# Four hand-overs between the stages of an image kernel, rearranged on one core

## The chip, the cores and the metric

The kernel runs on one core of a Trainium2 chip. The metric is the time of one execution on the device in microseconds (us); the median of several runs is compared. The engines go by their short names: PE multiplies matrices (PEld are its weight loads), DVE and POOL work elementwise, ACT computes functions, and SP does nothing here but issue DMA transfers. POOL and ACT issue transfers too, each in the order of its own instructions.

## What is computed

The input `x` is an image of 256 by 256 pixels with 128 channels, float32. Four layers follow each other, each of the form "x plus a layer of the group norm of x":

```
def _gn(v, G=32, eps=1e-5):                     # mean and variance per group of 4 channels, over all pixels
    ...
x = x + _L0_conv_ref(_gn(x), ...)   # attention along rows, 4 heads, with a bias from the pixels
x = x + _L1_conv_ref(_gn(x), ...)   # gated complex recurrence, 16 steps: h = fg * (A h) + inp
x = x + _L2_conv_ref(_gn(x), ...)   # triangle product: left, right = gated projections of layer norm
                                    #   out = einsum('bikd,bjkd->bijd', left, right / L)
                                    #   out = sigmoid(pair_norm @ g_out) * (layer_norm(out) @ p_out)
x = x + _L3_conv_ref(_gn(x), ...)   # 3 x 3 convolution, 128 to 128 channels, then a 128 x 128 product
```

A group norm needs sums over the whole image. So no layer can start before the one ahead of it has finished its last pixel, and each hand-over ends in a short chain of tiny operations.

## The kernel before

**Stages.** Images lie in DRAM with channels as rows (128 partitions) and pixels as columns: `x1T` after attention, `x2T` after the recurrence, `x3T` after the triangle layer. A Python loop writes out an order of steps for each stage, with a lag for each step (software pipelining), and `pin` keeps the instructions of that order. What is not pinned is placed by a scheduler.

**Group norm** (`group_affine`, `mean_variance`). While a stage runs, it adds up sums and sums of squares (about a shift) per channel in `stats`. At the hand-over `mean_variance` adds these (`mv`), scales them and takes the variance; a product with `group` (1/4 inside groups of four channels) gives the group mean `pm`; the spread of the channel means is added (`d`, `v`); a second product `pv` gives the group variance; ACT takes the root (`sd`), after loading its table; `ab` holds the factor and the offset of the norm. `keep_busy` puts products of no use between these, so that PE does not stand idle.

**Recurrence.** 64 blocks of 1024 pixels, in an order of steps with lags 0 to 4. The 16 steps are done in closed form by four squarings; the tail of a block is: `xa`, `xb` (three products add up `g`, twice `dn8` and minus `tq16` in `pxb`), `be`, `e_`, `al` on DVE, `t1` on POOL, and then two transfers `ac1`, `ac2` issued by POOL, which add `t1` and `yf` into the tile `xc`. ACT then takes the sums of `xc` (`ev_`, `bn`: four instructions), and `st` stores the block to `x2T`. After the last block `red` adds up the sums and `partps` folds the halves.

**Triangle layer.** A first pass over 32 tiles of 2048 pixels takes the layer norm, stores it (`znT`), keeps the roots as rows (`rs2D`), and fills the gated projections `LR` of a first quarter of the channels. Then for each of four quarters `g`: 32 channels of products `z`, their results stored to `prodD`, while the sums for the second layer norm are kept in `sums` and `total`. The buffers are `X[0]` to `X[4]`, 2048 columns each; in this pass `X[4]` holds `shift`, `total` and `v`. `fetch(g + 1, n)` loads the first four tiles for the next quarter.

After the last quarter: `total` minus `v`, logarithm, exponential, into `rsm`, written to `rs3D`; `transformed_taps` (called by `prepare`) multiplies the convolution's taps with the 128 x 128 matrix (`cpk`) and makes the six combinations `U` from them.

**Output stage.** 32 tiles of 2048 pixels. For each tile: `pa` spreads a row of roots over all partitions (`ra`), `xs` normalises on DVE, `e0` and `e1` are the products `pe` of the halves, `sg` their sigmoid, `pb` spreads the second row (`rb`), `sc` scales the loaded `pd`, `y0` and `y1` are the products `py`, `gy` gates, `ad` adds to `x` on POOL (the last tile on DVE), `qu` takes the squares, `st` stores to `x3T`. Steps of the tile before have lag 1:

```
order = (
     (lx, 0), (pa, 0), (y0, 1), (y1, 1), (xs, 0), (lp, 0), (gy, 1), (e0, 0), (pb, 0), (ad, 1),
     (sc, 0), (e1, 0), (sg, 0), (qu, 1), (st, 1),
)
```

**Convolution.** 16 blocks of 16 rows, by a transform along the rows (four rows of output from six `v`, groups of four rows). ACT applies the norm (`normalise`, into `xp`), DVE makes the six `v` (`transform`), PE multiplies (`products`, tiles `m`, one bank each of eight), DVE and ACT combine them (`rows`). Transform `gs` selects groups of a block; the first block is made in two halves.

The lines of the profile that are named below: L61 is every product, L55 every ACT function, L958, L961, L964, L1073 and L1087 are the recurrence's helpers and its transfers, L1119 is the pinned helper of the triangle layer, L1382 loads the rows of roots, L1400 the tiles `x` and `pd`, and L1588 to L1603 the transform.

Of the kernel before, what the change touches and what calls it, by code (L numbers as in the profile page):

```python
# [31 lines left out]
class Kernel:  # L32
# [50 lines left out]
    def group_affine(self, pool, psum, stats, group, tag, whole=False, shift=None, mv=None, busy=8):  # L83

        nc = self.nc
        if mv is None:
            mv = self.mean_variance(pool, stats, tag, shift)
        pin = self.tc.keep_in_program_order
        pm = psum.tile([P, 2], F32, name=f"pm{tag}", tag="gn")
        self.keep_busy(psum, busy)  # L90
        pin(self.mm(pm[:, 0:1], group, mv[:, 0:1]))
        self.keep_busy(psum, 3)
        mg = pool.tile([P, 1], F32, name=f"mg{tag}")
        nc.vector.tensor_copy(mg, pm[:, 0:1])
        d = pool.tile([P, 1], F32, name=f"gd{tag}")
        nc.vector.tensor_sub(d, mv[:, 0:1], mg)
        v = pool.tile([P, 1], F32, name=f"gv{tag}")
        nc.vector.scalar_tensor_tensor(v, d, d, mv[:, 1:2], ALU.mult, ALU.add)
        pv = psum.tile([P, 2], F32, name=f"pv{tag}", tag="gn")
        pin(self.mm(pv[:, 0:1], group, v))  # L100
        self.keep_busy(psum, 3)
        sd = pool.tile([P, 1], F32, name=f"sd{tag}")
        self.chain("table", self.act(sd, pv[:, 0:1], AF.Sqrt, bias=self.eps))
        ab = pool.tile([P, 2], F32, name=f"ab{tag}")
        nc.vector.reciprocal(ab[:, 0:1], sd)
        nc.vector.scalar_tensor_tensor(ab[:, 1:2], mg, -1.0, ab[:, 0:1], ALU.mult, ALU.mult)
        if whole:
            return ab, mg, sd
        return ab

    def mean_variance(self, pool, stats, tag, shift):

        nc = self.nc
        mv = pool.tile([P, 2], F32, name=f"mv{tag}")

        nc.vector.tensor_reduce(mv, stats, AX.X, ALU.add)
        nc.vector.tensor_scalar_mul(mv, mv, 1.0 / NPIX)
        e = pool.tile([P, 2], F32, name=f"me{tag}")
        nc.vector.tensor_tensor(e[:, 0:1], mv[:, 0:1], shift, ALU.add)
        nc.vector.tensor_tensor(e[:, 1:2], e[:, 0:1], e[:, 0:1], ALU.mult)  # L120
        nc.vector.tensor_tensor(mv[:, 1:2], mv[:, 1:2], e[:, 1:2], ALU.subtract)
        return mv
# [28 lines left out]
    def constants(self, pool):  # L151
# [4 lines left out]
        self.g4 = self.load(pool, self.i["c_group4"], "g4")  # L156
        self.eps = pool.tile([P, 1], F32, name="eps")
# [146 lines left out]
    def later_weights(self, pool):  # L304
# [14 lines left out]
        W["bv"] = self.column(pool, I["L3_conv_bias"], "bv")  # L319

# [10 lines left out]
    def attention(self, wp, later, xT, x1T, znT, biasD, HD_, stats1, shift1):  # L331
# [5 lines left out]
        with ExitStack() as c:  # L337
# [7 lines left out]
            with self.pool(name="awq", bufs=2, space=PSUM) as ps0:  # L345
                ab, mg, _ = self.group_affine(wp, ps0, None, self.g4, "0", True, mv=mv)
                V.tensor_scalar_mul(shift1, mg, -1.0)
                lc, cb = self.centering(wp, ps0, ab, "0")
# [521 lines left out]
    def recurrence(self, x1T, x2T, HD_, stats1, shift1, stats2, shift2):  # L870
# [7 lines left out]
        with ExitStack() as c:  # L878
# [8 lines left out]
            with self.pool(name="rwp", bufs=2, space=PSUM) as ps0:  # L887
                ab, mg, _ = self.group_affine(wp, ps0, stats1, self.g4, "1", True, shift=shift1)
# [170 lines left out]
            def xb(d): total(d, "pxb", [[(self.ident, d["g"]), (twice, d["dn8"]), (negid, d["tq16"])]])  # L1059
            def lD(d): act(d["D"], d["D"], AF.Ln)  # L1060
            def eD(d): act(d["D"], d["D"], AF.Exp, bias=math.log(0.5), scale=-1.0)
            def be(d): stt(d["g"], d["pxb"][:, 0], 2.0, d["D"], ADD, MUL)
# [7 lines left out]
            def t1(d): gt(wide(d, "t1"), both(d["t"]), d["v"], MUL)  # L1070
            def yb(d): tt(d["yf"], d["yf"], both(d["g"]), MUL)

            def added(d, t): pin(nc.gpsimd.dma_start(d["xc"], t, accum_op=ADD))  # L1073
# [26 lines left out]
            for it in range(NB + deep):  # L1100
                for step, lag in order:
                    if 0 <= it - lag < NB:
                        D[it - lag]["b"] = it - lag
                        step(D[it - lag])
            red = wp.tile([P, 2, 2], F32, name="partsum")
# [646 lines left out]
```

## Time and profile before

| | us |
|---|---|
| median of 3 runs (4716.51 to 4721.29) | 4718.13 |
| time of the profiled execution | 4713.07 |
| its span, first to last instruction | 4711.2 |
| PE busy in the span | 4538.0 |
| DVE busy | 3746.5 |
| ACT busy | 3332.6 |
| POOL busy | 2104.2 |

The hand-overs that the change touches, by windows of the trace:

| hand-over | window (us) | PE busy | DVE busy | ACT busy | POOL busy | granted clock |
|---|---|---|---|---|---|---|
| attention to recurrence | 1651 to 1658 | 6.08 of 7 | 4.66 | 2.36 | 0.56 | 1.00 |
| recurrence to triangle | 2962 to 2999 | 12.73 of 37 | 11.79 | 9.84 | 12.20 | 0.63 |
| products to output stage | 3847 to 3880 | 21.73 of 33 | 12.98 | 9.75 | 8.44 | 0.64 |
| output stage to convolution | 4174 to 4188 | 13.94 of 14 | 9.93 | 8.49 | 1.14 | 1.00 |

The profile records one execution; times in it count from its first instruction. "Busy" of PE includes products that serve only to keep it busy. The granted clock is the share of its full clock that PE was given in a window. A row of the timeline has the start, the length, the engine, the line, the operation, output and inputs with their shapes, the number of instructions put together, and in brackets how long the engine had stood idle and what released it. Every float32 product stands in the trace as two instructions.

### The profile page before, as it was taken

How to read it: one execution, taken by the hardware profiler on the slowest of the kernel's cores; microseconds unless marked ns; L12 is line 12 of the kernel's file. 1: busy time of each engine (PE TensorE's matmuls, PEld its weight loads, DVE VectorE, ACT ScalarE, POOL GpSimd, SP SyncE). 2: the span in 40 equal slices, each digit the busy share in tenths (PEclk: the TensorE clock that was granted, in tenths of full speed). 3: DMA queues.
4: the chain of work that ended last, by engine and by line, in shares of the span. 5: the costliest groups of instructions: out<-in, count | busy, mean ns of one | idle time of the engine just before them, and what ended most of it. 6: DMA issues, size and time to landing. Idle time of an engine off the chain costs nothing.

```text
span 4711.2 us, 79401 instructions
## 1 busy us (share of the span) xinstructions
PE 4538.0 (96%) x30421; PEld 2602.1 (55%) x30421; DVE 3746.5 (80%) x4818; ACT 3332.6 (71%) x5176; POOL 2104.2 (45%) x1365
## 2 busy tenths in 40 slices
PE   8999999999999999999999999799999989999999
PEld 2444555555555533333333333356999963379999
DVE  6776777777777789999999999687666667789885
ACT  6555888888888889999999999698444444442210
POOL 0343555555555547666767666333231145520000
PEclk9999999999999999999999999899999989999999
DMA  8893122222222235555555555576767758955332
GB/s 306 298 348 147 46 82 84 88 82 86 82 84 88 69 92 135 135 131 129 136 131 131 134 129 121 188 258 238 250 218 254 259 191 312 356 220 173 131 115 72
DMA packets 221194, 769.14 MB, mean 163 GB/s; under 512 B 58726, under 2 KB 62076, under 8 KB 180468
## 3 DMA queue, kind: packets, MB, share of 16 engines
q1 hardware_dynamic: 154542, 465.37, 28.9%
q0 software_dynamic: 64976, 298.27, 22.1%
q8 instruction: 243, 3.98, 0.3%
q14 instruction: 137, 1.12, 0.1%
q10 hardware_dynamic: 1296, 0.40, 0.0%
HBM read 431.26 MB, written 265.55 MB: 148 GB/s over the span
## 4 chain that ended last, share of the span: by engine, by line
PE 65%; ACT 15%; DVE 11%; issue 6%; DMA 2%; POOL 1%; SPq 0%; ACTq 0%; POOLq 0%; DVEq 0%
PE z L61 14%; PE m L61 8%; PE nd L61 7%; PE sc L61 6%; PE ppq L61 3%; PE ppv L61 3%; PE pe L61 3%; PE zc L61 2%; PE py L61 2%; PE ppg L61 2%; PE ppk L61 2%; PE px L61 2%; ACT L933 2%; PE pr L61 2%; ACT x2q L55 2%
## 5 line engine op out<-in xcount | busy, mean ns | idle before, releaser
L592 DVE TENSOR_TENSOR e<-sc,bT 128x1024 f32<-128x1024 f32 x512 | 613.8, 1220 | 255.5 <-PE sc L61 253.4
L592 POOL TENSOR_TENSOR ks<-e 128x1024 f32<-128x1024 f32 x256 | 601.4, 2368 | 442.6 <-PE nd L61 429.2
L55 ACT ACTIVATE e<-e 128x1024 f32<-128x1024 f32 x512 | 539.4, 1054 | 39.1 <-DVE e L592 29.5
L61 PE MATMUL m<-U,v 128*128 128x128 f32 x4608 | 514.8, 275 | 0.0
L61 PEld LDWEIGHTS m<-U,v 128*128 128x128 f32 x4608 | 514.6, 192 | 0.0
L61 PEld LDWEIGHTS z<-wf,zt 128*128 128x128 f32 x4096 | 462.6, 192 | 54.0 <-DVE LR L1119 28.5
L61 PE MATMUL z<-wf,zt 128*128 128x128 f32 x4096 | 474.8, 277 | 6.0 <-DVE LR L1119 6.0
L1119 DVE TENSOR_TENSOR LR<-z,sg 128x512 f32<-128x512 f32 (+1 forms) x323 | 270.0, 867 | 165.5 <-ACT sg L55 165.5
L1119 POOL TENSOR_TENSOR zt<-zt,df 128x512 f32<-128x512 f32 x127 | 161.5, 1272 | 422.8 <-ACT df L55 422.6
L55 ACT ACTIVATE sg<-z 128x512 f32<-128x512 f32 (+1 forms) x323 | 160.9, 509 | 243.7 <-PE z L61 241.4
L61 PE MATMUL sc<-proj 32*128 32x256 f32 x4096 | 299.8, 403 | 3.2 <-DVE e L592 2.3
L961 POOL TENSOR_TENSOR fs<-f 128x512 f32<-128x512 f32 x64 | 176.3, 2755 | 275.4 <-DVE f L958 255.8
L61 PEld LDWEIGHTS sc<-proj 32*128 32x128 f32 x4096 | 187.9, 185 | 160.8 <-PE px L61 94.8
L61 PE MATMUL nd<-e,proj 128*32 128x256 f32 x4096 | 272.4, 384 | 2.6 <-DVE og L592 2.6
L55 ACT ACTIVATE dn<-dn 128x512 f32<-128x512 f32 x384 | 237.7, 619 | 10.3 <-DVE dn L592 6.3
L961 POOL TENSOR_TENSOR u<-t,tr 128x512 f32<-128x512 f32 x64 | 232.4, 3631 | 12.1 <-DVE tr L964 10.6
L961 POOL TENSOR_TENSOR t<-t,v 128x1024 f32<-128x1024 f32 x64 | 210.1, 3283 | 54.4 <-DVE t L958 54.4
L61 PE MATMUL z<-LR 128*128 128x256 f32 x1024 | 225.5, 383 | 7.5 <-DVE LR L1119 7.5
L1637 POOL DMA_DIRECT2D out_dram<-ys x32 | 37.0, 1157 | 424.2 <-DVE ys L1635 424.2
L1627 ACT COPY m4s<-m 128x512 f32<-128x512 f32 x32 | 18.7, 583 | 287.3 <-PE m L61 287.3
L61 PEld LDWEIGHTS z<-LR 128*128 128x128 f32 x1024 | 196.6, 192 | 35.6 <-DVE LR L1119 8.3
L1119 POOL TENSOR_TENSOR x<-ga,x 128x1024 f32<-128x1024 f32 x62 | 144.7, 2350 | 133.8 <-DVE ga L1119 133.8
(410 smaller groups left out, 10749.0 us busy)
## 6 DMA issues: line engine op xcount, KB each, us to landing
zt<-znT SPq DMA_DIRECT2D x96, 1024.0 KB
xin<-in_x_dram SPq DMA_DIRECT2D x48, 1024.0 KB
xr<-x3T SPq DMA_DIRECT2D x46, 768.0 KB
x1T<-x POOLq DMA_DIRECT2D x64, 512.0 KB, 4.9
xf<-x1T SPq DMA_DIRECT2D x64, 512.0 KB
xc<-x1T SPq DMA_DIRECT2D x128, 256.0 KB
xc<-t POOLq DMA_DIRECT2D x64, 512.0 KB, 4.6
xc<-yf POOLq DMA_DIRECT2D x64, 512.0 KB, 5.0
```

The costliest lines, as they stand in the source:

```text
L55: return self.nc.scalar.activation(out, in_, func, bias=bias, scale=scale, **kw)
L61: return self.nc.tensor.matmul(out, lhsT, rhs, start=start, stop=stop)
L592: pin = lambda f: lambda *a, **k: tc.keep_in_program_order(f(*a, **k))
L933: pin(nc.scalar.preload_act_table_set(want))
L961: pin(nc.gpsimd.tensor_tensor(out, a, b_, op))
L1119: pin = lambda f: lambda *a, **k: tc.keep_in_program_order(f(*a, **k))
L1627: nc.scalar.copy(m4, m[4])
L1637: nc.gpsimd.dma_start(out[row:row + 8].rearrange("r p t c -> p (r t) c"), ys.rearrange("p g k t c -> p (g k t) c"))
```

## The change

- **Group norms.** For the recurrence, the triangle layer and the convolution, one product of the raw sums with `g4n` (the group matrix divided by the number of pixels) gives both group means at once; the variance is taken from them on DVE. Scaling, one product and several tiny operations are gone. The first group norm stays as it was.
- **Recurrence.** For the last block alone, `xb` is done by two DVE operations, `t1` on DVE, and `ac1` and `ac2` are additions on DVE. After the loop stand 56 products of no use (`warm`).
- **Taps.** The products of the taps (`cpb`, `cpk`) move from the output stage's beginning to the triangle layer's (`tap_products`), in place of 11 products of no use; the copies go from ACT to DVE. `transformed_taps` keeps only DVE's combinations; it is called between steps of the output stage's first tile.
- **Output stage.** `fetch` of the last quarter loads the first four tiles of `x2T` into `X[0]` to `X[3]`, and the first row of roots into `X[4]` (`root`); the stage then goes on using `X`. The row of `rb` for the first tile comes from `v` in SBUF by four small transfers of POOL and ACT; the write of `rs3D` and the rows of tiles 1 to 3 follow. In the first tile `e1` comes ahead of `pb`. The last tile's `gy` and `ad` alternate by halves.
- **Convolution.** The first block is transformed in groups 0, 1 and then 2 and 3; DVE does three of the first six rows of its `xp`; the first half's products go group by group. Fewer products of no use stand ahead of it (22 and 13 for 26 and 26).

By the order of instructions of both kernels: DVE's queue has, in the last product steps of the triangle layer, two of the tap combinations between its additions, two more between the halves of the first `xs`, and the other nine ahead of the first `sc`. POOL's queue has two loads of rows between its last additions and two after them. SP's queue has the first `pd` ahead of the last store to `prodD`, and waits for `rs3D` ahead of `pd` 2 and 3.

```diff
+    self.g4n = pool.tile([P, P], F32, name="g4n")
+    nc.vector.tensor_scalar_mul(self.g4n, self.g4, 1.0 / NPIX)
...
+            V.tensor_reduce(mv, stats, AX.X, ALU.add)
+            self.keep_busy(psum, busy)
+            pin(self.mm(pm, self.g4n, mv))
+            self.keep_busy(psum, 3)
+            V.tensor_tensor(d, pm[:, 0:1], shift, ALU.add)
+            V.scalar_tensor_tensor(v, d, d, pm[:, 1:2], ALU.mult, ALU.subtract)
+            V.tensor_copy(mg, pm[:, 0:1])
+            self.chain("table", self.act(sd, v, AF.Sqrt, bias=self.eps, scale=-1.0))
...
+            def last(d): return d["b"] == NB - 1
+            def xb(d):
+                if last(d):
+                    stt(thin(d, "tr8"), d["dn8"], -2.0, d["tq16"], MUL, ADD)
+                    tt(d["g"], d["g"], d["tr8"], SUB)
+                else:
+                    total(d, "pxb", [[(self.ident, d["g"]), (twice, d["dn8"]), (negid, d["tq16"])]])
...
-            def t1(d): gt(wide(d, "t1"), both(d["t"]), d["v"], MUL)
+            def t1(d): (tt if last(d) else gt)(wide(d, "t1"), both(d["t"]), d["v"], MUL)
...
+            def added(d, t):
+                if last(d):
+                    tt(d["xc"], d["xc"], t, ADD)
+                else:
+                    pin(nc.gpsimd.dma_start(d["xc"], t, accum_op=ADD))
...
+            for _ in range(56):
+                pin(self.mm(warm[:, 0, :P], self.ident, self.cmat))
...
-                ab, mg, _ = self.group_affine(wp, ps0, stats2, self.g4, "2", True, shift=shift2, busy=11)
+                self.tap_products(ps0)
+                ab, mg, _ = self.group_affine(wp, ps0, stats2, "2", shift=shift2, busy=0)
...
                 def fetch(g, n):
-                    if g < G:
-                        zt[g, n] = X[n % 4]
-                        nc.sync.dma_start(zt[g, n], znT[:, n * 2048:(n + 1) * 2048])
+                    zt[g, n] = X[n % 4]
+                    nc.sync.dma_start(zt[g, n], (znT if g < G else x2T)[:, n * 2048:(n + 1) * 2048])
+                root = X[4][:, 1536:]
...
+                        if g == G - 1:
+                            nc.sync.dma_start(root[32 * n:32 * n + 1], rs2D[:, n * 512:(n + 1) * 512])
...
-                nc.gpsimd.dma_start(rs3D[0].rearrange("(p n) -> p n", p=P), rsm.rearrange("p a j b -> p (a j b)"))
-            quarters.close()
-            prepare(W["kt"], W["wd"], W["bv"])
...
-                for p in range(4):
-                    D[p]["p"] = p
-                    load_x(D[p])
                 roots(0, "ra", rs2D, nc.gpsimd)
-                roots(0, "rb", rs3D, nc.gpsimd)
+                R["rb", 0] = io.tile([P, 4, 512], F32, name="rb")
+                for k in range(4):
+                    (nc.gpsimd, nc.scalar)[k % 2].dma_start(R["rb", 0][32 * k:32 * k + 1, 0], v[k:k + 1])
+                nc.gpsimd.dma_start(rs3D[0].rearrange("(p n) -> p n", p=P), v)
+                for k in range(4):
+                    nc.gpsimd.dma_start(R["rb", 0][32 * k:32 * k + 1, 1:], rs3D[0].rearrange("(p k n) -> k p n", k=4, n=512)[k:k + 1, 1:4])
...
+                first = [(step, lag) for step, lag in order if not lag]
+                cut = next(n for n, (step, lag) in enumerate(first) if step is pb)
+                e1_at = next(n for n, (step, lag) in enumerate(first) if step is e1)
+                first.insert(cut, first.pop(e1_at))
...
+                            if not it and step is pb:
+                                prepare()
...
+    def tap_products(self, ps):
+        W, V = self.weights, self.nc.vector
+        kt, wd = W["kt"], W["wd"]
+        pb = ps.tile([P, 2], F32, name="cpb", tag="gn")
+        self.mm(pb[:, 0:1], wd, W["bv"])
+        V.tensor_copy(W["bw"], pb[:, 0:1])
+        for t in range(3):
+            pk = ps.tile([P, 3, P], F32, name="cpk")
+            for n in range(3):
+                self.mm(pk[:, n], kt[:, 3 * t + n, :], wd)
+            V.tensor_copy(kt[:, 3 * t:3 * t + 3, :], pk)
...
+                if blk == 0:
+                    s, t = parts[0]
+                    V.tensor_scalar(xp[:, (s + t) // 2:t, 1:N + 1], xr[:, (s + t) // 2:t, :], ab[:, 0:1], ab[:, 1:2], MUL, ADD)
+                    parts = [(s, (s + t) // 2), *parts[1:]]
...
+                one_by_one = blk + half == 0
+                for g, i in [(g, i) for g in range(2) for i in order] if one_by_one else [(None, i) for i in order]:
...
-            for gs in (slice(0, 2), slice(2, 4)):
+            for gs in (slice(0, 1), slice(1, 2), slice(2, 4)):
```

## The prediction

> **What bounds the kernel now.** I read the page first (busy shares and the slices of part 2), then the chain of waits in order of time to find where the tensor engine is not the thing that ends last, then the timeline and the clock windows of those places alone.
>
> ```profile
> span 4711.2 us, 79401 instructions
> PE 4538.0 (96%) x30421; PEld 2602.1 (55%) x30421; DVE 3746.5 (80%) x4818; ACT 3332.6 (71%) x5176; POOL 2104.2 (45%) x1365
> PEclk9999999999999999999999999899999989999999
> ```
>
> PE is busy 96% of the span, so nothing that shortens another engine inside a stage is worth much. The granted clock has two dips (slices 26 and 33): the hand-overs from recurrence to triangle and from its products to its output stage. All edits sit at hand-overs, so I cost four of them: A (1651 us, into the recurrence), B (2962 to 2999, out of it), C (3847 to 3880, into the output stage), D (4174 to 4188, into the convolution). From the timeline:
>
> ```profile
> 2968.95 0.86 POOL L1073 DMA_DIRECT2D xc<-yf  x1 [4.11 <-DMA xc<-t]
> 2973.86 3.26 POOL L961 TENSOR_TENSOR t<-t,v 128x1024 f32<-128x1024 f32 x1 [2.78 <-DVE t L958]
> 2982.45 0.86 POOL L1073 DMA_DIRECT2D xc<-yf  x1 [4.09 <-DMA xc<-t]
> 2987.24 0.63 ACT L55 ACTIVATE x2q<-xc 128x512 f32<-128x512 f32 x1 [10.32 <-issue]
> 2990.44 0.42 DVE L1106 TENSOR_REDUCE partsum<-parts 128x4 f32<-128x256 f32 x1 [15.53 <-ACT x2q L55]
> 2999.12 1.06 PE L61 MATMUL mn<-zt,tmeana 128*32 128x512 f32 x8 [0.25 <-DVE twbe L1154]
> 3862.77 3.69 PE L61 MATMUL ra<-ra,tones 1*128 1x512 f32 x8 [7.59 <-DMA ra<-rs2D]
> 3866.61 3.75 PE L61 MATMUL pe<-xs,twe 128*128 128x512 f32 x4 [0.15 <-DVE xs L1119]
> 3879.86 3.70 PE L61 MATMUL py<-pd,two 128*128 128x512 f32 x8
> 4181.94 4.57 ACT L55 ACTIVATE xp<-xr,ab 128x1536 f32<-128x1536 f32 x3 [0.77 <-DMA x3T<-x]
> 4187.84 27.33 PE L61 MATMUL m<-U,v 128*128 128x128 f32 x243
> ```
>
> B: the last block walks through POOL, two accumulating transfers and four ACT sums before anything can be normalised. C: PE waits for a row that lands 7.4 us after its issue, then works slowly up to the first py; from there py follows py every 9.4 us with PE full. D: the first xp ends two waits together, the coefficients `ab` (4181.71 + 0.16) and the last store (4177.77 + its 4.1 us to landing = 4181.9); products start 5.9 us later. The clock, by windows:
>
> ```profile
> 2960.00:2962.00 2.00, 1.94 (x5) 0.57 (x3) 1.19 (x3) 0.73 (x2) 0.75 (x1) 1.00 0.00 0
> 2962.00:2964.00 2.00, 0.00 (x0) 0.00 (x0) 2.00 (x2) 0.00 (x0) 1.70 (x2) 1.00 0.00 0
> 2964.00:2966.00 2.00, 0.00 (x0) 0.00 (x0) 1.97 (x4) 1.73 (x4) 0.84 (x1) 0.52 0.33 66
> 3876.00:3878.00 2.00, 2.00 (x4) 0.67 (x2) 0.40 (x1) 0.00 (x0) 0.00 (x0) 0.50 1.02 430
> 3878.00:3880.00 2.00, 2.00 (x10) 0.46 (x10) 0.02 (x1) 1.11 (x1) 0.00 (x0) 0.79 0.99 418
> 3974.00:4068.00 94.00, 94.00 (x321) 34.96 (x321) 73.20 (x80) 44.86 (x62) 52.32 (x30) 1.00 0.94 357
> ```
>
> (Columns: window, length, busy of PE, its loads, DVE, ACT, POOL; clock, DMA share, GB/s.) The clock is 1 or one half. A mean of 0.52 puts a fall at 2964.1, 0.79 a rise at 3878.8.
>
> **A: group norm of the recurrence.** On the path from the reduce at 1652.49: the scaling (0.17), one product stage (pv, 0.38), a copy and the waits between are gone; one product gives both columns, then two small DVE operations, then the root. Row by row: pm ends 1653.35, gd 1653.56, gv 1653.80; the root's table is there at 1653.75, so sd runs at 1653.85 instead of 1654.69. **0.8 us**. An xf/xc load or HD row could hide it: 0 to 1.
>
> **B: last block on DVE.** From xa at 2965.92: tr, g, be, e_, al are five DVE operations of 512 columns at 0.72 in a chain (pxb and its slow PE pass, 2966.66 to 2971.6, are gone), so al ends at 2970.1; t1, the first sum, yb and the second sum are four of 1024 columns at 1.24: xc is ready at 2975.1. But block 62 still goes by transfer: its sums start at 2973.75 and take four times 0.8, to 2976.95; those of block 63 follow to 2980.2. The reduce comes at 2980.2, not 2990.44: 10.2. Removed too: t1 on POOL, two DMA issues on its queue; stores move up. Behind it: the 56 warming products are 112 instructions of 0.112 (the 52 of 5.81 us), 2962 to 2974.5, so 6 us short; the clock falls before 2980. partps then runs at 2980.7, and the tap products now lie ahead of pm: 20 instructions and 2 of tpw at 0.213 (half clock) for 3.4 to 5.1 us, pm at 2985.5 to 2986.1. In before the filler cost the same (partps 2990.91, pm 2995.47). The three kt copies (0.47 each) on DVE end about with them. From pm to `ab` 1.5 instead of 2.2. Sum: first mn near 2988.9 instead of 2999.1: **10.2 us**, bounds 9 to 12. The first x2T tile is no wait: issued at the end of partps as before, and the rows of before leave it 7.8 us.
>
> **C: output stage.** Tiles 0 to 3 and the first root row lie in SBUF before the last z (3847.4). The chain is now: the sums, delayed about 0.5 by two tap operations and two row issues (0.52 each) put between DVE's and POOL's last additions; total minus v, which stands ahead of xs on DVE, ends at 3852.9 (was 3852.45); xs first half to 3854.2; two U operations (0.65); second half to 3856.1. pe first and second half now run back to back from 3854.3. Between ra (3849 to 3850) and this PE stands 4 us. [...] rb's row: v is ready at 3854.5; POOL issues two parts by 3855.7, ACT two after its table load by 3857. The trace bounds the landing by 4.2 us (x3T, quiet queues) and 8.2 (rb of before, crowded): 3860 to 3864; only pd tiles 0 and 1 move then, so 3861. U's remaining nine operations (4.5 us at 0.47 to 0.55) end on DVE at 3861: hidden by the row. rb to 3862.1, sc halves to 3864.1, ra of tile 1, py at 3863.2 instead of 3879.86: 16.7. Against it: rb of tile 1 comes by the rs3D round trip, write issued at 3856.3, landing 4.4 to 7.1 later, POOL's four issues, 4.2 to 8.2 more, wanted at 3868.6: 0 to 5 us, I take 0.7; SP waits for the same write ahead of pd 2 and 3, which are wanted only near 3880; and light windows may drop the clock once: 0.5. **15.5 us**, bounds 9 to 17.5. Copies of kw on ACT and the cpk pass (4 us) lay under the row's wait already: nothing.
>
> **D: into the convolution.** Interleaving makes DVE's last four operations end at 4176.96 instead of 4177.46; the last store is issued and lands 0.5 earlier, 4181.4. The group norm is shorter, `ab` at 4181.1, but xp must overwrite tiles that this store reads, as before, so 4181.4 stands. DVE: four U updates to 4182.05, its half of xp (768 columns, 0.55 by the rows of TENSOR_SCALAR), then tb, ta, tg, v at 258 columns, 0.34 each (516 take 0.61): first product 4184.1 instead of 4187.84, 3.7. Given back: DVE needs 24 small operations (8.2 us) for what took 12 (7.3); the second half's third and fifth bank are freed by the row sums of the first, and walking both queues row by row PE waits 1.3 us there. After that the 4608 m instructions run at 0.112. **2.4 us**, bounds 0 to 4.
>
> Sum: 0.8 + 10.2 + 15.5 + 2.4 = 28.9. The profiled execution took 4713.07 (span plus 1.9), so it would take 4684.2; the median of the three runs is 5.1 higher: 4718.1 - 28.9 = 4689.2, say 4689. About 0.2% (9.4 us) is what a measurement here can tell from no change.
>
> **The rivals.**
>
> Wait takes the place of wait (0.25): the rows for rb land as in the crowded row (8.2 us: 3864) and tile 1 waits for rs3D; PE is idle again, falls to half clock and does the first py slowly. C is then 9, D perhaps 1: total 21, 4697. For: 7.1 to 8.2 are this seam's own rows. Against: the four 1 MB tiles that crowded it are gone.
>
> Hand-back in several seams (0.07): B's statistics wait on block 62 longer, D is zero since the store decides. Total 12 to 18, near 4703. For: two of D's three waits end in that store. Against: PE, not the store, carries the 5.9 us after it.
>
> Everything warm (0.05): the clock holds, 33 or more, 4684.
>
> It does not do what it says (0.02): if SP held the x2T loads until the last z, tile 0 would land about 4.2 us after 3848.5, when xs is due anyway (3852.9), and the root row by its 7.4 at 3855.9: 3 us less, still the main case. Only if both long seams ended in a wait outside these rows would A and D be left, 3 us: 4715, inside 9.4.
>
> Slower (0.03): the output stage becomes transfer bound. It moves some 99 MB (32 x 3.15 less four tiles, plus xr); PE needs 32 x 9.4 = 301 us, so 329 GB/s. The middle stretch shows a DMA share of 0.94 at 357. If the new queue order, with pd 2 and 3 behind the rs3D wait, kept them below 293 GB/s, the stage would take 339 us and eat the gain and 9 more: about 4728. Against: PE is 94.00 of 94 there, 430 GB/s occurs, and four tiles leave the stage.
>
> Main case 0.58, total 24 to 33.
>
> **Numbers.** 4689 is the main case's. The range 4682 to 4700 takes in its bounds and the first rival, leaving out the hand-back's and slower ends. Faster 0.95 (all but the last two cases and the fringe), same 0.02, slower 0.03.
>
> **What would show it.** Right: the reduce of partsum 10 us closer to the last av; no row on POOL for block 63; pe back to back and the clock back to 1 before the first py; py about 16 us after the last z instead of 32; m about 14 us after the last py begins, instead of 17.6. Wrong: a DMA releaser of several us ahead of rb, a clock of 0.50 under py, m with holes in the first two blocks, or a py period above 9.4.

## The result and the profile after

| | before | changed |
|---|---|---|
| median, 4 runs each | 4717.32 (4714.15 to 4721.29) | 4687.17 (4686.27 to 4692.74) |
| profiled execution, its span | 4713.07, 4711.2 | 4687.51, 4685.7 |
| a second profile of each, its span | 4712.30, 4710.4 | 4682.89, 4681.1 |

The ratio is 0.9938, interval 0.9921 to 0.9955: 30.2 us less by the medians, where 28.9 was forecast. The two pairs of profiles give 25.5 and 29.3.

From the page of the changed kernel, its span, engine shares and clock slices:

```profile
span 4685.7 us, 79549 instructions
PE 4524.4 (97%) x30447; PEld 2603.2 (56%) x30447; DVE 3753.2 (80%) x4828; ACT 3329.8 (71%) x5173; POOL 2099.7 (45%) x1364
PEclk9999999999999999999999999999999999999999
```

The two dips of the clock are gone from the slices; falls of 6.8 us remain at both seams (2979.32 to 2986.15, 3842.89 to 3849.72), as shown below. The seams, in the timeline of the changed kernel:

```profile
2963.43 12.67 PE L61 MATMUL warm<-cmat,ident 128*128 128x128 f32 x112
2970.61 0.86 POOL L1077 DMA_DIRECT2D xc<-yf  x1 [4.11 <-DVE g L958]
2975.52 1.22 DVE L952 TENSOR_TENSOR xc<-xc,yf 128x1024 f32<-128x1024 f32 x1
2975.54 0.63 ACT L55 ACTIVATE x2q<-xc 128x512 f32<-128x512 f32 x1 [7.46 <-issue]
2981.95 0.42 DVE L1113 TENSOR_REDUCE partsum<-parts 128x4 f32<-128x256 f32 x1 [5.20 <-ACT x2q L55]
2990.02 1.07 PE L61 MATMUL mn<-zt,tmeana 128*32 128x512 f32 x8 [0.25 <-DVE twbe L1162]
...
3843.20 2.19 PE L61 MATMUL ra<-zt,tones 1*128 1x512 f32 x8 [4.81 <-ACT zt L55]
3846.67 5.20 PE L61 MATMUL pe<-xs,twe 128*128 128x512 f32 x8 [1.27 <-DVE xs L1126]
3852.55 1.32 PE L61 MATMUL rb<-rb,tones 1*128 1x512 f32 x6 [0.69 <-DMA rb<-zt]
3855.09 3.70 PE L61 MATMUL py<-pd,two 128*128 128x512 f32 x8
...
4151.22 5.18 PE L61 MATMUL busy<-cmat,ident 128*128 128x128 f32 x44 [2.20 <-DVE ga L1126]
4156.24 0.28 PE L61 MATMUL pm<-mv,g4n 128*128 128x2 f32 x2
4157.05 1.28 ACT L55 ACT_TABLE_LOAD   x1 [3.34 <-DVE mg L97]
4159.87 1.07 DVE L1591 TENSOR_SCALAR xp<-xr,ab 128x768 f32<-128x768 f32 x1
4162.34 3.28 PE L61 MATMUL m<-U,v 128*128 128x128 f32 x27 [1.46 <-DVE v L1613]
```

Block 63 has no row on POOL (2970.61 is the last transfer of block 62), and its last sum (2975.52 to 2976.74) is hidden behind block 62's statistics. PE waits 0.69 us for the row of `rb`, where it had waited 7.59 for that of `ra`. In D, PE's fillers and not the store now stand in front.

Seam by seam, both profiles of each kernel (C and D run to and from the start of a `py`; D ends with the start of the first `m`):

| stretch | before | changed | gain forecast | measured |
|---|---|---|---|---|
| A: reduce of `mv` to first `za` | 4.59, 4.60 | 3.77, 3.77 | 0.8 | 0.8 |
| A: the same reduce to first `av` | 39.86, 39.65 | 39.90, 39.92 | 0.8 | -0.2 |
| start of last but one to start of last `av` | 19.15, 19.21 | 22.01, 19.06 | 0 | -2.9, 0.2 |
| B: end of last `av` to first `mn` | 37.18, 37.29 | 26.43, 26.41 | 10.2 | 10.8 |
| C: end of last `z` to first `py` | 32.51, 33.26 | 16.69, 16.56 | 15.5 | 16.3 |
| first to last `py` | 290.34, 290.34 | 290.34, 290.34 | 0 (0.7 and 0.5 taken off in C) | 0 |
| D: last `py` to first `m` | 17.64, 17.64 | 16.91, 16.91 | 3.7 | 0.7 |
| first `m` to the end | 523.33, 523.32 | 523.40, 523.39 | -1.3 | -0.1 |

### The profile page after: what moved, and what is told of

It is laid out like the page before. It is cut to its first block, busy times and chain, and to the rows that moved or that the text cites. A ratio compares the mean times of both kernels' runs of the same rounds, so it can differ in the third digit from the quotient of the medians.

```text
span 4685.7 us, 79549 instructions
## 1 busy us (share of the span) xinstructions
PE 4524.4 (97%) x30447; PEld 2603.2 (56%) x30447; DVE 3753.2 (80%) x4828; ACT 3329.8 (71%) x5173; POOL 2099.7 (45%) x1364
## 5 line engine op out<-in xcount | busy, mean ns | idle before, releaser
L55 ACT ACTIVATE e<-e 128x1024 f32<-128x1024 f32 x512 | 539.4, 1054 | 39.2 <-DVE e L586 29.6
L1126 DVE TENSOR_TENSOR LR<-z,sg 128x512 f32<-128x512 f32 (+1 forms) x323 | 269.9, 866 | 165.4 <-ACT sg L55 165.4
L1126 POOL TENSOR_TENSOR zt<-zt,df 128x512 f32<-128x512 f32 x127 | 161.2, 1270 | 423.4 <-ACT df L55 423.4
L55 ACT ACTIVATE sg<-z 128x512 f32<-128x512 f32 (+1 forms) x323 | 160.7, 509 | 244.3 <-PE z L61 242.0
L55 ACT ACTIVATE dn<-dn 128x512 f32<-128x512 f32 x384 | 238.0, 620 | 10.2 <-DVE dn L586 6.1
L955 POOL TENSOR_TENSOR u<-t,tr 128x512 f32<-128x512 f32 x64 | 237.0, 3704 | 10.9 <-DVE tr L958 9.8
L1126 POOL TENSOR_TENSOR zt<-ga,zt 128x1024 f32<-128x1024 f32 x62 | 144.7, 2351 | 117.5 <-DVE ga L1126 117.5
```

Of the source, the lines that this page charges most:

```text
L55: return self.nc.scalar.activation(out, in_, func, bias=bias, scale=scale, **kw)
L955: pin(nc.gpsimd.tensor_tensor(out, a, b_, op))
L1126: pin = lambda f: lambda *a, **k: tc.keep_in_program_order(f(*a, **k))
```

## The experiments

Each run is the changed kernel with the edits that are shown or named, and its ratio is to the kernel before on the same chip; its seams are read from one profile. In the edits, `...` stands for what is left out. Below, "the changed kernel's" values are those of the table.

**B undone.**

```
-            def last(d): return d["b"] == NB - 1
+            def last(d): return False
-            warm = ...; for _ in range(56): ...
```

> The changed kernel, but the last block of the recurrence is finished as all others (pxb product, t1 on POOL, two accumulating transfers) and without the 56 warming products. Theory (the chain of the last block ends 10 us earlier, seam B carries 10.8 us): the reduce of partsum comes 15 to 18 us after the last av instead of 12.4 us earlier than that sum would have it, the first mn 37 us after the last av instead of 26.4, total slower than the changed kernel by 9 to 11 us, ratio to the kernel before about 0.996. Rival (statistics of block 62, which still go by transfer, set the end anyway, and the gain in B came from the shorter group norm): the first mn moves back by 3 us or less. On the recurrence itself, which took 4.2 us more in the changed kernel's profile than before: if the edits of the last block lengthen its drain, start of za to end of the last av returns from 1309.0 to about 1304.9; if it was only the phase in which the clock fell, it lies anywhere between 1303 and 1310.

Measured: 4702.46 (14 runs), ratio 0.9976 (0.9968 to 0.9984). The reduce of `partsum` came 28.84 us after the last `av` (18.36), not at 15 to 18 as written beforehand; in the kernel before it was 28.5. The first `mn` came 38.76 after it (26.43): B is worth 12.3 against a kernel that keeps everything else, 1.5 more than against the kernel before. Of the 1.5, 0.3 lie ahead of the reduce; for the rest the likely cause is that the tap products now stand in this seam, ahead of `pm`. The rival is out. The last `av` came 22.52 us after the one before, with the tail undone: the 2.9 us that the first profile lost there don't come from the edit. Over all twelve profiles with A changed this interval is either 19.06 to 19.22 (7 times) or 22.0 to 22.7 (5 times), and the same program gave 22.01 and 19.06: it varies from execution to execution. The clock goes with it: within this interval it was at half for 3.4 us in all seven short ones and in both profiles of before, and for 10.2 to 13.2 us in all five long ones. A window of the changed kernel's first profile, and the same of its second:

```profile
2952.00:2960.00 8.00, 4.77 (x9) 1.89 (x8) 5.39 (x6) 2.90 (x7) 1.71 (x3) 0.79 0.59 133
2952.00:2960.00 8.00, 6.64 (x19) 3.29 (x20) 6.56 (x10) 3.75 (x8) 1.77 (x3) 1.00 0.59 133
```

(Columns as in the prediction's windows; the clock is the third number from the end.) What starts the longer fall stays open. In the tail-undone profile the output stage took 6.4 us more too, of which below.

**C, tiles fetched late.**

```
-                        fetch(g + 1, n)      # and the rows of root, for the last quarter
+                        if g < G - 1: fetch(g + 1, n)
...
+                for n in range(4): pin(nc.sync.dma_start)(root[32 * n:32 * n + 1], ...)
+                for n in range(4): pin(nc.sync.dma_start)(X[n], x2T[...])
```

> The changed kernel, but the first four tiles of x2T and the first row of roots are fetched by SP after the last store of prodD, instead of a quarter ahead. With the tiles late, the scheduler also puts all combinations of taps ahead of the first xs on DVE. Theory of the prediction's second-last case (tile and row land about when xs is due anyway): first py 3 to 5 us later than in the changed kernel (19.7 to 21.7 us after the last z instead of 16.7). Rival (the early fetch is what seam C lives from): row and tile land 7 to 8 us after their issue, PE falls to half clock, first py 10 us or more later.

Measured: 4694.89 (6 runs), ratio 0.9961 (0.9949 to 0.9974). First `py` 23.14 us after the last `z`, 6.5 later, and 5.3 more lost in the first two tiles: 11.8 in all. In the timeline of this kernel:

```profile
3842.63 2.86 PE L61 MATMUL ra<-zt,tones 1*128 1x512 f32 x8 [6.01 <-DMA zt<-rs2D]
3858.48 2.35 DVE L1126 TENSOR_TENSOR pd<-pd,rb 128x1024 f32<-128x1024 f32 x2 [9.00 <-DMA pd<-prodD]
3859.76 6.52 PE L61 MATMUL py<-pd,two 128*128 128x512 f32 x8 [3.67 <-DVE pd L1126]
```

`ra` starts only 1.2 us later than in the changed kernel (idle 6.01 for 4.81). The first `xs` then begins 10.4 us after the last `z` for 6.9, straight behind the tap combinations, which the scheduler put ahead of it here. What the prediction missed is the next wait: the four tiles of 1 MB are issued ahead of the second part of the first `pd`, DVE waits 9.00 us for it, PE stands 3.67 us, and `py` runs at half clock (6.52 for 3.70). So early fetch carries most of C. How much of the 11.8 is the 4 MB in the way of `pd` and how much the changed order on DVE, this run does not separate. Neither theory had either.

**C, row of `rb` by the round trip.**

```
-                    (nc.gpsimd, nc.scalar)[k % 2].dma_start(R["rb", 0][32 * k:32 * k + 1, 0], v[k:k + 1])
...
-                    ... R["rb", 0][32 * k:32 * k + 1, 1:], rs3D[0]...[k:k + 1, 1:4]
+                    ... R["rb", 0][32 * k:32 * k + 1], rs3D[0]...[k:k + 1, 0:4]
```

> The changed kernel, but the row of rb for the first tile comes through rs3D as before: write, then four loads, all on POOL. Theory (the row is what PE waits for last in seam C, so its route is on the path): write lands about 5.3 us after its issue, loads 5 to 8 us after theirs, the row at about 3858 to 3860 on the changed kernel's scale instead of 3852.55: first py 6 to 10 us later, with the clock at half under it since PE then stands idle for over 5 us. Rival (the round trip is hidden by xs, pe and the combinations of taps on DVE): first py at most 2 us later.

Measured: 4693.82 (5 runs), ratio 0.9961 (0.9947 to 0.9975). PE waited 2.33 us for the row, first `py` 19.39 us after the last `z`, 2.7 later: between the 6 to 10 of the theory and the 2 of the rival. Then that `py` took 6.72 instead of 3.70, so 5.7 in all. The route is on the path, but half of its price is the clock. The write took its 5.3 us; the loads, for which I had 5 to 8, were there 2.4 us after the first was issued.

**D, fewer fillers; B, more warming.**

```
-  self.group_affine(..., "3", shift=shift3, busy=22)     +  busy=4
-            for _ in range(56):                          +            for _ in range(80):
```

> The changed kernel with two edits at two seams: 4 instead of 22 products of no use ahead of the group norm of the convolution (seam D), and 80 instead of 56 warming products after the recurrence (seam B). D, theory (the fillers wait for a PSUM bank that the last gy holds, start 2.2 us late and stand in front of pm): pm about 2 us earlier, first m 14.7 to 15.2 us after the last py begins instead of 16.9. D, rival (the last store's landing at 4156.9 or the load of the root's table decides): first m moves by 0.3 us or less. B, theory (the clock falls at 2979.7 because PE stands idle for 6.3 us after the warming products): with 80 the clock stays at full, the tap products take 0.113 each instead of 0.15 to 0.21, first mn 24.7 to 25.2 us after the last av instead of 26.4. B, rival (DVE's copies and statistics set pm): 0.3 us or less.

Measured: 4685.91 (4 runs), ratio 0.9945 (0.9928 to 0.9961). D: `pm` 8.65 us after the last `py` begins (10.81), first `m` 15.15 (16.91), as the theory has it. The late-fetch kernel adds to it: there, from the same source line, the 44 filler instructions began at once behind the last `py`, without the wait for `ga`, and `m` came at 14.91. B: first `mn` 24.71 us after the last `av` (26.43), also as the theory has it. But that gain was given back: from the last `av` to the last `z` it was 874.21 (first profile of the changed kernel 874.81, second 874.28).

**C, rows of tiles 1 to 3 from `v`; D, table ahead.**

```
-  nc.gpsimd.dma_start(R["rb", 0][32 * k:32 * k + 1, 1:], rs3D[0].rearrange(...)[k:k + 1, 1:4])
+  nc.gpsimd.dma_start(R["rb", 0][32 * k:32 * k + 1, 1:], v[4 + k:16:4])
...
+  tc.keep_in_program_order(self.table("sqrt_and_others"))      # ahead of the convolution's group norm
```

> The run with 4 fillers and 80 warming products, and two edits more. Seam C: the rows of rb for tiles 1 to 3 come straight from v in SBUF as tile 0's does, not through rs3D. Theory (two of four executions with this code lost 3 to 6 us in the first two tiles of the output stage, because the row of tile 1 came late by the round trip or PE then fell to half clock): the rows land within 6 us of their issue, before 3856 on the changed kernel's scale, every py period is 9.4, 290.3 us from first to last py. Rival (the loss comes from the phase of the clock windows alone): a period of 12 or more can still occur. Seam D: the table of the root is loaded ahead of the group norm. Theory (load and root stand between gv and ab, 1.3 us): ab 1.2 us earlier, and then the last store's landing, 4.1 us after its issue, sets xp: first m 14.0 to 14.3 us after the last py begins instead of 15.15. Rival (the updates of U and the DVE half of xp set the end, the table does not): 15.0 or more.

Measured: 4684.5 (4 runs), ratio 0.9932 (0.9911 to 0.9954). No wait for a row, all periods 9.4. D: 15.28, no gain on the 15.15 of the run with 4 fillers and 80 warming products, though the root (`sd`) was done 1.3 us before the reciprocal ran. The timeline of this kernel:

```profile
4154.22 0.29 ACT L55 ACTIVATE sd<-gv,eps 128x1 f32<-128x1 f32 x1 [0.20 <-DVE mg L97]
4155.64 0.29 DVE L1571 COPY bw<-cpbw 128x128 f32<-128x128 f32 x1 [1.12 <-PE cpbw L61]
4155.85 0.15 DVE L111 RECIPROCAL ab<-sd 128x1 f32<-128x1 f32 x1
```

The reciprocal is queued on DVE behind a copy that waits for PE: the wait removed on ACT is replaced by one that had lain under it.

**C, `e1` behind `pb`; D, first block in two groups (with 4 fillers).**

```
-                first.insert(cut, first.pop(e1_at))
...
-            for gs in (slice(0, 1), slice(1, 2), slice(2, 4)):
+            for gs in (slice(0, 2), slice(2, 4)):
```

> The changed kernel with 4 fillers, and two parts undone at two seams. Seam C: e1 of the first tile after pb, as in the other tiles. Theory (in the changed kernel the second half of pe fills the wait for the row of rb): PE stands idle for about 3 us ahead of rb, half clock follows, first py 1.7 to 5 us later than 16.7. Rival (pe of the second half fits under the scaling of pd just as well): within 0.5 us. Seam D: the first block of the convolution in two groups of two, as before, products not group by group. Theory: tb, ta, tg and v at 516 columns take 0.6 each instead of 0.34, first m 1.0 to 1.2 us later than 15.15, the rest of the stage unchanged (523.4). The prediction's give-back (PE waits 1.3 us in the first block for the small groups): the rest of the stage gets shorter by 1 us or more, the sum of both unchanged.

Measured, one run: 4695.5. C: 22.25, 5.6 later, more than the theory's 5; PE waits 2.46 us for the row, then the second half of `pe` runs at half clock behind it (3.78 for 4 instructions). D: first `m` at 17.07, 1.9 later than 15.15, and the rest of the stage unchanged (523.39). The operations of 516 columns cost 0.61 each, and the scheduler put one other (`tc`) among the four, ahead of the `v` that the first `m` waits for. So the small groups bring 1.9 with that order, and the give-back of 1.3 doesn't exist.

**D, first `xp` on ACT alone (with 4 fillers).** The five lines of `if blk == 0:` in `normalise` are left out.

> The changed kernel with 4 fillers, and all of the first xp on ACT as before (DVE's half undone). Theory (DVE's half takes 1.07, not 0.55, and stands behind the updates of U, so ACT alone would be done as early): first m within 0.3 us of 15.15 after the last py begins. The prediction's reckoning (half of it on DVE at 0.55): first m 0.7 to 1 us later.

Measured, one run: 4683.56; first `m` at 15.11, for 15.15 with DVE's half. That part of the change brought nothing there.

**All of it, and both kernels again.** Beside the edits of the last runs, the tap combinations are pinned behind `xs`, the fillers are 11, and the copy of `bw` follows the updates of `U`.

```
-            V.tensor_tensor(e, k0, k2, ADD)        +            pin(V.tensor_tensor(e, k0, k2, ADD))   # and so on
+            tc.add_manual_dep(V.tensor_copy(bw, pbw).ins, upd.ins.name, NOSYNC, reason="bw")
```

> All that the runs so far point to, in the changed kernel: 80 warming products; rows of rb for tiles 1 to 3 straight from v; the combinations of taps pinned behind both halves of the first xs, so that none of them delays the last sums; 11 fillers ahead of the group norm of the convolution (they then end about when its statistics are ready), the table of the root loaded ahead, and the copy of the convolution's bias product behind the updates of U, so that it no longer stands in front of ab on DVE. Theory: B 24.7 us from the last av to the first mn (26.4 in the changed kernel), C 15.4 to 15.9 from the last z to the first py (16.7), D 14.0 to 14.5 from the last py to the first m (16.9): 5 to 5.5 us faster than the changed kernel, median about 4682 on the scale where that has 4687, ratio 0.9988. Rival (the rb row and the last store set C and D whatever DVE and ACT do): C 16.5, D 15.2, 3.5 us faster.

> The changed kernel once more, unaltered, for a second profile and a median beside the run before it. Seams as in its first profile (A 3.8, B 26.4 to 26.6, C 16.5 to 17, D 16.9). The recurrence, start of za to end of the last av: anywhere in 1305 to 1311 if the phase of the clock sets its drain; within 1 us of the first profile's 1309.0 if the program sets it. Output stage from first to last py: 290.3, or up to 6 us more if the row of the second tile comes late.

> The kernel before once more, unaltered, for a second profile. If the recurrence's length varies from execution to execution by the phase of the clock, it differs from the first profile's 1304.86 by more than 0.5 us, and lies within 1304 to 1311 like those of the changed one; if the changed kernel made it longer, it is again 1304.5 to 1305.3. Seams B 37.2, C 32.5 and D 17.6, each within 0.5 us except C, where the clock was at half and may move it by up to 3 us.

Measured on one chip: 4681.43 (4679.71 to 4683.46, 5 runs) for the version with all edits, ratio to before 0.9929 (0.9916 to 0.9943); 4684.88 (4682.89 to 4688.07, 5 runs) for the changed kernel again, 0.9938 (0.9924 to 0.9951). It is 3.4 us faster by the medians, within what the two overlapping intervals leave open. B 24.73, C 15.46 and D 14.39 came as expected, 5.4 together, but the first tiles of the triangle layer took 2.8 longer. The timeline of this version behind its first `mn`, and windows of the clock:

```profile
2983.80 1.07 PE L61 MATMUL mn<-zt,tmeana 128*32 128x512 f32 x8 [0.25 <-DVE twbe L1162]
2985.63 2.09 PE L61 MATMUL pr<-mr,tspread 32*128 32x512 f32 x8 [0.77 <-ACT mr L55]
2987.65 1.94 PE L61 MATMUL mn<-zt,tmeana 128*32 128x512 f32 x8
```

```profile
2984.00:2986.00 2.00, 1.24 (x12) 0.37 (x8) 0.00 (x0) 0.60 (x1) 0.00 (x0) 0.79 1.00 422
2986.00:2988.00 2.00, 2.00 (x12) 0.35 (x12) 0.24 (x1) 0.00 (x0) 0.00 (x0) 0.50 1.03 434
```

With 56 warming products the clock falls under the wait and is back up for these tiles (`pr` 1.14 in the changed kernel's second profile, all windows of 2984 to 2998 at 1.00); with 80 it holds through the seam and falls at about 2985.2, under the tiles: fourth `mn` 19.9 us after the first instead of 17.1. In D the last wait is now the store (`xp` on ACT: `[1.90 <-DMA x3T<-zt]`).

The recurrence of the kernel before took 1304.29 in its second profile (first 1304.86), 0.6 less: too little to show by itself that it varies there; both have the short last interval. The changed kernel's second took 1305.68 for 1309.04, and has it short now. So of the 4.2 us that its first profile lost between first `za` and last `av`, 2.9 are that interval in one execution, and 0.8 are A's, below. In the ten profiles with A changed and no products added there, the same stretch took 1305.3 to 1311.1, so two profiles of before are too few to say that the change costs nothing there.

**The clock at A and B.** Three products of no use more at A; then 80 warming products and three more at B.

```
                 ab, mg, _ = self.group_affine(wp, ps0, stats1, "1", shift=shift1)
+                self.keep_busy(ps0, 2)
...
                     V.tensor_scalar_mul(gw[g], raw, ab[:, 0:1])
+                self.keep_busy(ps0, 1)
```

> The version with all edits, with 56 warming products again, and three products of no use more at seam A: two after those behind pm, one ahead of the first za, where PE waits 0.5 and 0.3 us. In all profiles of the changed kernel the way from the statistics' reduce at A to the first av took 39.7 to 40.3 us, as before (39.7 and 39.9): the 0.8 us of the shorter group norm were lost again, za taking 1.7 instead of 1.1 and m 3.8 instead of 3.4 at half clock. Theory (with one product stage gone, its fillers are gone too, and the clock falls near 1655 instead of 1660): with three more products the clock holds to 1658 or beyond, first av 39.0 to 39.3 us after the reduce. Rival (a wait of the first blocks for HD rows or ACT sets the first av): 39.7 or more. At B: 26.4 to the first mn, and 874.3 us from the last av to the last z, 1 us less than the 875.3 of the version with all edits. Total 1 to 2 us below that version.

> As the run with three more products at A, but with 80 warming products, and two more of no use ahead of pc and one ahead of the first mn. In the three runs with 80 warming products the first mn came 1.7 us earlier, and the last z no earlier (874.2 to 875.3 us after the last av, against 872.9 to 874.8): the clock fell near 2985, under the first tiles. Theory (the window before 2985 holds too little full-width work; three products of 0.23 raise it): the clock stays at full under the first three tiles, fourth mn 17.1 us after the first, 872.5 to 873 us from the last av to the last z. Rival (three products are too few, or the fall comes later instead): fourth mn 18 to 20 us after the first, 874 to 875.5.

Measured on one chip (before: 4711.10): 4681.42 (4680.72 to 4684.0, 5 runs) and 4684.15 (4677.92 to 4694.31, 5 runs), both ratio 0.9938 (0.9924 to 0.9951 and 0.9952). Windows of the clock at A, first of the kernel before, then of the changed kernel's first profile, then of the first run with three more products:

```profile
1660.00:1662.00 2.00, 2.00 (x4) 0.42 (x2) 0.00 (x0) 1.51 (x2) 0.00 (x0) 0.55 0.06 9
```

```profile
1654.00:1656.00 2.00, 1.70 (x13) 0.46 (x10) 0.77 (x6) 0.00 (x0) 0.00 (x0) 0.74 0.59 191
1656.00:1658.00 2.00, 0.86 (x3) 0.50 (x2) 0.00 (x0) 1.66 (x2) 0.00 (x0) 0.50 0.06 7
1658.00:1660.00 2.00, 2.00 (x3) 0.68 (x2) 0.00 (x0) 1.56 (x2) 0.00 (x0) 0.50 0.04 4
```

```profile
1654.00:1656.00 2.00, 1.08 (x5) 0.25 (x4) 0.12 (x2) 0.84 (x1) 0.00 (x0) 1.00 0.24 65
1656.00:1658.00 2.00, 1.77 (x4) 0.68 (x4) 0.00 (x0) 1.98 (x3) 0.00 (x0) 1.00 0.05 5
1658.00:1660.00 2.00, 2.00 (x11) 0.71 (x12) 0.00 (x0) 1.62 (x3) 0.00 (x0) 1.00 0.25 54
```

In the first run the first `av` came 37.05 us after the reduce instead of 39.9, 2.9 us earlier than in the changed kernel and 2 more than its theory had. The second run has the same three products, and there it came 44.11 us after the reduce:

```profile
1656.85 3.68 PE L61 MATMUL busy<-cmat,ident 128*128 128x128 f32 x16 [2.86 <-issue]
```

PE stood 2.86 us for nothing that the profile shows, and the clock was at half from 1657.0 on under these fillers (1.95 us in the changed kernel). From the first `za` to the first `av` it took 35.8 us there, 33.0 in the first run and 36.1 in the changed kernel. So the gain of 2.9 is one profile's, and not repeated. In the kernel before the clock fell too, at about 1660.2.

At B the second run had its fourth `mn` 17.1 us after the first, with the first at 24.42: the clock held. But the last `z` came 875.7 after the last `av`, not 872.5 to 873: from the fourth `mn` to the last `z` it took 834.2 us, for 831.3 and 830.8 in the changed kernel, and the clock fell three times for 3.4 us there, for two times in those. The first run missed its figures for B as well (first `mn` 26.91, last `z` 878.7). In the totals no gain shows: both profiles had a long last interval of the recurrence (22.6, 22.7), the first fell under the triangle layer's first tiles (fourth `mn` at 19.7), and both under the first `py` (5.3 for 3.7); the second's execution was the slowest of its five. Which of these versions is the fastest stays open.

## Why the prediction was right, and where not

**Total.** The main case came, but that 28.9 lies so near 30.2 is in part luck, since errors cancel: by the means of both profiles B and C brought 27.1 for a forecast of 25.7, A and D 0.6 for 3.2. The spans of the profiles differ by 27.4 on average, and the stretches add up to that: 27.7 at the four seams and 2.0 from attention's end, less 1.8 between first and last `av` and 0.4 in the triangle layer. No edit aims at attention's end: its last statistics came 1.7 and 2.3 us earlier than in both profiles of before (1652.49), but over the other profiles with the change at anything between 1649.4 and 1655.7. Whether the edits move it stays open; what the medians show beyond 27.4 is in no profile.

**A.** The step "so sd runs at 1653.85 instead of 1654.69: 0.8" was right, its place on the path was not. The stage removed had taken its fillers with it, and the clock fell near 1655 instead of 1660: 4.2 us behind the reduce instead of 7.7. `za` and `m` lost what the norm had won. I had costed the removed fillers at nothing and looked for the cover in transfers. That the fillers are the cause rests on the windows and on one profile with three of them put back; the other profile, with its stall, does not show it.

**B.** The chain came as worked out: reduce 10.1 earlier, set by block 62's statistics and then block 63's, as forecast. They began 4.9 us after the transfer's issue at 2970.61, and DVE was done while they ran. The clock fell at about 2979.3, in the wait, as forecast:

```profile
2978.00:2980.00 2.00, 0.00 (x0) 0.00 (x0) 0.00 (x0) 1.94 (x5) 0.24 (x1) 0.83 0.85 262
```

It came back at about 2986.15, so the tap products ran at half clock for 3.4 us (from 2982.73), where the forecast had 3.4 to 5.1.

That the last block's chain carries B, and not the shorter group norm, is shown by the run with the tail undone, for the chain and the warming products together. The norm's own part was not tried alone.

**C.** The clock fell at about 3842.9, `pe` began at half clock and took 5.20 for eight instructions, and the clock was back to 1 at about 3849.7, before the first `py` (3855.09), as forecast.

```profile
3842.00:3844.00 2.00, 0.80 (x4) 0.61 (x8) 0.00 (x0) 1.94 (x3) 1.19 (x1) 0.72 0.62 189
```

The prediction has PE stand 4 us behind `ra`; it stood 1.3 there (3845.39 to 3846.67). `ra` was placed 1.7 us behind the last `z` and came 4.8 behind it (`[4.81 <-ACT zt L55]`), so PE stood still ahead of `ra` and not only behind it, 4.5 us by the time of the fall. In the kernel before, the fall at 2964.1 had come 2.1 us after the end of PE's last product (2961.94). In the first run with three more products at A it fell at about 3838.7, 2.0 us after the last `z` had ended at 3836.65:

```profile
3836.00:3838.00 2.00, 0.65 (x3) 0.22 (x2) 1.31 (x3) 1.35 (x4) 1.68 (x2) 1.00 0.94 193
3838.00:3840.00 2.00, 0.00 (x0) 0.00 (x0) 1.22 (x2) 0.65 (x2) 1.80 (x3) 0.67 0.64 213
```

So at these three falls PE had stood still for 2.0 to 4.5 us. In the changed kernel the clock came back 3.0 us after `pe` began. Mis-sized: the two tap operations and issues delay the sums by 1.3 us, not 0.5, since DVE's `e` and `h` took 0.92 and 1.06 beside POOL's addition, for 0.56 and 0.36 in the kernel before; with them pinned away C was 1.1 shorter. The row of `rb` landed 14.2 us after the last `z`, for 13.6 forecast. The terms 0.7 and 0.5, for tile 1's row and for the clock, are averages over cases that either come or don't. The 0.5 was the author's estimate, and no run shows it; in its place, in the five profiles with seam C as changed the way from first to last `py` is 290.3 four times, and 296.7 once (tail undone). The rival "does not do what it says" was under-priced: late tiles cost 11.8 us, not 3.

**D.** Forecast 2.4, measured 0.7. The failing step is "`ab` at 4181.1 [...] so 4181.4 stands", that the store decides. Counted from the start of the last `py`, the store landed as forecast (11.45 us for 11.2), but `ab` came at 13.65 for 10.9. The step left out the fillers. In the kernel before the `gy` of the first half released them, 3.4 us after that start:

```profile
4173.53 5.88 PEld L61 LDWEIGHTS busy<-cmat,ident 128*128 128x128 f32 x52 [0.57 <-DVE ga L1119]
```

In the changed kernel they waited for the last `gy` (`[2.20 <-DVE ga L1126]`), which the interleaved `ad` had put 0.8 us later, and began after 5.8 us. 44 instructions of 0.113 then stood ahead of `pm`, whose sums had been ready for 2.2 us; the run with 4 fillers brought 1.8 back. That the wait is for the PSUM bank that this `gy` reads was inferred: the late-fetch kernel, with the same lines, did not have it. Second, "its half of xp 0.55" was 1.07 and worth nothing. Third, the table load, which lay under waits before, stands in front of `sd`. Against these, the small groups brought 1.9, not 1.1, and cost nothing. In the versions with 11 fillers, the table ahead and the copy moved the store does decide, as the step had it: with the same edits at D, the first `m` came at 14.38 and at 15.07 in the two runs with three more products at A, the store having landed 4.13 and 4.82 us after its issue.

## What to carry to other kernels

When a stage of a short chain goes, count the filler that goes with it, and ask what the clock does behind it: at A it fell 4.2 us behind the reduce instead of 7.7. A seam's gain is only real at the next full pipeline step, not at the first instruction behind it. Measure a seam by anchors (last product of one stage, first and fourth of the next), in two profiles: between the two profiles of the same kernel the seams here repeat within 0.8 us, most within 0.2, and the total of the changed kernel doesn't within 5. And ask of every filler which buffer it needs, and who still reads that.

## What the runs showed of the hardware

The clock fell with PE busy almost without a gap. In the run with three more products at A, around its first `py` at 3852.53:

```profile
3850.05 1.14 PE L61 MATMUL rb<-rb,tones 1*128 1x512 f32 x8
3851.01 1.44 PE L61 MATMUL ra<-ra,tones 1*128 1x512 f32 x8
3852.53 5.29 PE L61 MATMUL py<-pd,two 128*128 128x512 f32 x8
```

```profile
3848.53:3850.53 2.00, 2.00 (x8) 0.71 (x10) 1.52 (x4) 0.75 (x2) 0.00 (x0) 0.90 1.11 329
3850.53:3852.53 2.00, 1.92 (x17) 0.69 (x9) 1.28 (x2) 0.74 (x1) 0.00 (x0) 0.95 0.23 46
3852.53:3854.53 2.00, 2.00 (x3) 0.97 (x4) 2.00 (x2) 0.00 (x0) 0.00 (x0) 0.50 0.55 90
```

PE was busy 1.92 of the 2 us ahead of the fall, but with products of one input row. So the clock fell here, at about 3852.3, with no wait of PE ahead of it in the rows. The tail-undone run agrees: it lost 6.4 us although PE waited only 0.25 us for the second `rb`. That products of few rows are the cause was inferred from these windows, not tried by itself. Two smaller things. In the changed kernel's first profile a row of 2 KB from SBUF took 5.7 us to land while 66 to 295 GB/s moved, one of 6 KB from DRAM 2.0 us when little else did (0 to 131 GB/s); but in two other profiles (tail undone, rows from `v`) the first such row of 2 KB landed in 1.8 us, while 16 to 165 GB/s moved. And TENSOR_SCALAR with two operands on 768 columns took 1.07 us, near the 1.22 of 1024 columns of a two-tensor operation, not the 0.55 read off the smaller rows.
